# A gated cross-attention and mixture block on one core: attention's transposes moved up a step, the shared PSUM bank handed out in turn with a gap, and the mixture's transposes moved to other banks

## The chip, the core and the metric

The kernel runs on one NeuronCore of a Trainium2 chip. The metric is device time in microseconds (us) of one execution; the time before is 1071.58 us, the median of three runs (1070.88 to 1074.14). Five engines work side by side, each through its own list of instructions in a fixed order: TensorE (PE, matmul), VectorE (DVE), ScalarE (ACT), GpSimd (POOL) and SyncE (SP, which here issues nearly all DMAs). An instruction waits until what it reads is written and what it overwrites has been read; everything behind it in the same engine's list waits with it.

## What is computed

Eight sequences of 256 tokens with 512 features pass through two gated blocks in float32. The first is attention with 32 query heads, 8 key heads and a window of 64 tokens over two sources, the normed input and a context; one softmax runs over both. The second is a feed forward whose eight "basis" pieces are mixed per token with coefficients from a top-4 router, plus a shared part.

```python
x = x + tanh(g_xattn) * attention(layernorm(x), ctx)      # scores + alibi bias, masked to the window
xt = layernorm(x)
probs = softmax(xt @ w_router); topk_p, topk_idx = top_k(probs, 4)
basis = silu(xt @ w_gate) * (xt @ w_up)                   # 8 pieces of 256 columns
mixed = sum over experts and pieces of coeff * mix[topk_idx] * basis
out = mixed @ w_down + (silu(xt @ shared_w_gate) * (xt @ shared_w_up)) @ shared_w_down
x = x + tanh(g_ffn) * out
```

## The kernel before

One sequence is called b. Its work is four generators, and each `yield` hands back a cost. `project(b)` loads x and the context, norms x, transposes it in two halves (`tr_x`, L160), and makes keys (`pk`, L366), queries (`pq`, L385) and values (`pv`, L405). `attention(b)` has eight groups of scores; `score(i)` writes group i into four PSUM banks (`sc`, L444), one for each of four pairs of heads p. A group is worked off in two halves j; the running number of a half is u = 2i + j. `soften` (L457 on DVE, L466 on ACT) adds the bias, takes the maximum and exponentiates, once for each p. `divide` (a reciprocal L473 on DVE, four products L476 on POOL) normalises half u - 1, `turn` (L484 on DVE) transposes half u - 2 into `pt`, and `values` (L506) multiplies four turned halves with a block-diagonal copy of the values, `vbd`, into unused columns of score banks; `take` (L523, ACT) copies that out. `tail(b, t)` runs for each half t of the tokens: output projection `po` (L610), residual, norm, transposes `tr_f` (L160), router `pl` (L640), top-4 selection, `pst` (L672), `pc` (L680), which yields the mixing coefficients. `feed_forward(b)` does the eight pieces: plain products `gu` (L725) for b = 0, and for b > 0 seven half-size block products `m` (L788) in place of eight, from sums of weights kept in DRAM; then the shared part `ps` (L894), the transposes of the mixed result `pm` (L926) and the last product `pd` (L941).

The order of work is written by a small planner, not by the hardware: `start` gives a generator a time at which it begins (in units of one sequence) and a length; `run` always advances the one with the earliest time, and every instruction goes to its engine's list at that moment. In the steady state feed_forward(b), attention(b + 1), the tails of b + 1 and project(b + 2) are interleaved.

PSUM is shared out thus: four banks hold scores (`ps_sc`), three go round for the feed forward (`next_bank`), and one, `ps_one`, serves project (from b = 2 on), the tails and `pm` in turn. A generator that wants `ps_one` calls `hold` and yields until `held` is false. Since the bank is single, an instruction that writes the next tile into it waits for the one that reads the last tile out. For `tr_x` that reader is an ACT copy (L161), which stands in ACT's list among the exponentials of attention.

SP issues DMAs in list order: weight pieces `w` (L292), sixteen DMAs for `vbd` (L539) in each sequence, the output (L952).

Of the kernel before, what the change touches and what calls it, by code (L numbers as in the profile page):

```python
# [9 lines left out]
F32 = mybir.dt.float32  # L10
# [26 lines left out]
def gated_block(  # L37
# [43 lines left out]
        return ps_gu.tile([P, 2, T], F32, tag=f"gu{turns[0] % 3}", name=name)  # L81


    held = [False]

    def hold():
        while held[0]:
            yield 0.4
        held[0] = True


    loaded = {}
# [219 lines left out]

    AFTER, BEFORE = 1.8, 1.2
    projected = {}

    def project(b):
        def own():
            if b > 1:  # L320
                yield from hold()

        def bank(shape, name):
            if b > 1:
                return ps_one.tile(shape, F32, tag="one", name=name)

            flat = next_bank(name).rearrange("p a n -> p (a n)")
            if len(shape) == 2:
                return flat[:, : shape[1]]
            if len(shape) == 3:  # L330
                return flat.rearrange("p (a n) -> p a n", a=shape[1])
            return flat.rearrange("p (a b n) -> p a b n", a=shape[1], b=shape[2])

        def free():
            if b > 1:
                held[0] = False

        if b > 1:
            while b > 2 and b - 3 not in stored:
                yield 0.5  # L340
            loaded[b] = load(b), load_context(b)
            yield 16.0
        xt, ctT = loaded[b]
        if b == 0:
            xns = first_normed
        else:
            normed = norm(xt, range(NT), f"a{b}")
            yield 3.0
            xns = normed()
            yield 3.0  # L350
        xnT = two.tile([P, NC, T], F32, tag="xo", name=f"xnT_{b}")
        for t in range(NT):
            yield from own()
            evict = transposed(xnT, xns[t], t, f"x{b}", bank)
            yield AFTER
            evict()
            free()
            yield BEFORE


        kT = two.tile([P, 2, 2, T], F32, tag="kT", name=f"kT_{b}")
        yield from own()
        pk = bank([P, 2, T], f"pk_{b}")
        for s, (w_sb, src) in enumerate(((wsk_sb, ctT), (wk_sb, xnT))):
            for c in range(NC):
                nc.tensor.matmul(  # L366
                    pk[:, s, :], lhsT=w_sb[:, c, :], rhs=src[:, c, :],
                    start=(c == 0), stop=(c == NC - 1),
                )
            yield AFTER  # L370
        for par in range(2):
            for s in range(2):
                nc.scalar.activation(
                    kT[:, par, s, :], pk[:, s, :], AF.Copy, scale=kmask[:, par : par + 1],
                )
        free()
        yield BEFORE


        qT = two.tile([P, NB, G, Q], F32, tag="qT", name=f"qT_{b}")  # L380
        for g in range(G):
            yield from own()
            pq = bank([P, T], f"pq_{b}_{g}")
            for c in range(2 * NC):
                nc.tensor.matmul(  # L385
                    pq, lhsT=wq_sb[:, c, g * P : (g + 1) * P],
                    rhs=(ctT if c < NC else xnT)[:, c % NC, :],
                    start=(c == 0), stop=(c == 2 * NC - 1),
                )
                if c % NC == NC - 1:  # L390
                    yield AFTER
            nc.scalar.activation(
                qT[:, :, g, :], pq.rearrange("p (b q) -> p b q", q=Q), AF.Copy, scale=-0.25
            )
            free()
            yield BEFORE
        projected[b] = kT, qT


        yield from own()  # L400
        pv = bank([P, NT, 2, HK * D], f"pv_{b}")
        for t in range(NT):
            for s, (w_sb, src) in enumerate(((wsv_sb, ctT), (wv_sb, xnT))):
                for c in range(NC):
                    nc.tensor.matmul(  # L405
                        pv[:, t, s, :], lhsT=src[:, c, t * P : (t + 1) * P], rhs=w_sb[:, c, :],
                        start=(c == 0), stop=(c == NC - 1),
                    )
            yield AFTER
        nc.scalar.copy(  # L410
            vpad[:, :, D:].rearrange("p a (k r) -> p a k r", r=2 * D)[:, :, :, :D],
            pv.rearrange("p t s (k d) -> p (t s) k d", d=D),
        )
        free()
        yield BEFORE


    def attention(b):
# [112 lines left out]
        for u in range(2 * n + 4):  # L531
# [24 lines left out]
                nmax = small.tile([P, NPAIR], F32, tag="nmax", name=f"nm_{b}_{u}")  # L556
                dens[u] = small.tile([P, NPAIR], F32, tag="den", name=f"dn_{b}_{u}")
            yield 1.0
            for step, ps in enumerate(((0,), (1, 2), (3,))):
                for p in ps:  # L560
                    if i < n:
                        soften(i, j, p, scs, prs[u], nmax, dens[u])
                if step == 1 and j == 1 and m is not None:
                    take(m, scs)
                    if m == n // 4 - 1:
                        start(tail(b, 0, oT), 0.30, total=37.0)
                if step == 0 and 0 <= u - 1 < 2 * n:
                    divide((u - 1) // 2, (u - 1) % 2, prs[u - 1], dens.pop(u - 1))
                if step == 2 and 0 <= u - 2 < 2 * n:
                    k = (u - 2) // 4  # L570
                    if (u - 2) % 4 == 0:
                        pts[k] = two.tile(
                            [P, P // Q, NPAIR, COLS], F32, tag="pt", name=f"pt_{b}_{k}"
                        )
                    turn(u - 2, prs.pop(u - 2), pts[k])
                if u < 2 * n + 2:
                    yield 1.0 if i < n else 0.5
        start(tail(b, 1, oT), 0.31 if b > 0 else 0.26, total=37.0)
        yield 0.1


    hTs, coef = {}, {}

    sides = {}

# [14 lines left out]
    def tail(b, t, oT):  # L600
# [3 lines left out]
        n = f"{b}_{t}"  # L604
        xt, _ = loaded[b]
        yield 2.0
        yield from hold()
        po = bank([P, HID], f"po_{n}")
        for ch in range(4):
# [6 lines left out]
            out=xt[:, t, :], in0=po, scalar=tg[:, 0:1], in1=xt[:, t, :],  # L616
            op0=ALU.mult, op1=ALU.add,
        )
        held[0] = False
        normed = norm(xt, [t], f"f{b}")  # L620
        yield 2.5
        (xn,) = normed()
# [5 lines left out]
        evict = transposed(hT, xn, t, f"f{b}", bank)  # L628
        yield 2.5
        evict()  # L630
        held[0] = False
        yield 2.5
        if t == NT - 1 and b > 0:
            sides[b] = token_sums(b, hT)

# [13 lines left out]
        nc.gpsimd.memset(prob[:, E:], -1.0)  # L649
        den = small.tile([P, 1], F32, tag="rdn", name=f"rdn_{n}")  # L650
        nc.scalar.activation(prob[:, :E], pl, AF.Exp, bias=nmax, scale=1.0, accum_out=den)
        held[0] = False
        yield 2.5
        rden = small.tile([P, 1], F32, tag="rrd", name=f"rrd_{n}")
        nc.vector.reciprocal(rden, den)
# [17 lines left out]
        yield 2.5  # L673
        selT = one.tile([P, P], F32, tag="selT", name=f"selT_{n}")
        nc.scalar.copy(selT, pst)
        held[0] = False
        yield 1.5
        yield from hold()
        pc = bank([P, NK], f"pc_{n}")
# [1 line left out]
        yield 2.5  # L681
        cf = small.tile([P, NK], F32, tag="cf", name=f"cf_{n}")
        nc.vector.tensor_scalar(cf, pc, rts, None, op0=ALU.mult)
        held[0] = False
        coef[b, t] = cf
        yield 0.0

# [12 lines left out]
    def feed_forward(b):  # L700
        while b > 0 and b - 1 not in stored:
            yield 0.2
        hT = hTs[b]
        xt, _ = loaded.pop(b)
        mixed = [one.tile([P, I], F32, tag=f"mixed{t}", name=f"mixed_{b}_{t}") for t in range(NT)]
        ths, ups, todo = {}, {}, []

# [44 lines left out]
        if b == 0:  # L752

            order = [(0, 0), (1, 0), (0, 1), (1, 1)]
            order += [(k, t) for k in range(2, NK) for t in range(NT)]
            for k, t in order:
                plain(k, t)
                while len(todo) > 1:
                    todo.pop(0)()
# [21 lines left out]
            }  # L781
            weights_of = {1: (1, 0), 5: (1, 1), 2: (2, 0), 6: (2, 1), 7: (3, 0), 3: (4, 0), 4: (4, 1)}

        def product(k, m, dst, first=False):
            g, j = weights_of[m]
            w = wgu[b * PIECES + k, g]
            for c in range(NC // 2):
# [14 lines left out]

        def one_and_five(k):
            odd[k] = next_bank(f"m15_{b}_{k}")
            product(k, 1, odd[k][:, 0, :], first=True)
            product(k, 5, odd[k][:, 1, :])
            after(b * PIECES + k, 1)

        def keep_one_and_five(k):
# [2 lines left out]

        def seven_and_six(k):
            even[k] = next_bank(f"m76_{b}_{k}")
            product(k, 7, even[k][:, 0, :], first=True)
            product(k, 6, even[k][:, 1, :])
            after(b * PIECES + k, 3)

        def keep_seven(k):
# [4 lines left out]
            nc.gpsimd.tensor_add(m7, m7, tiles.pop(("m5", k)))  # L824

        def two_and_three(k):
            product(k, 2, odd[k][:, 0, :])
            product(k, 3, odd[k][:, 1, :])
            after(b * PIECES + k, 2)

        def first_tile(k):
# [2 lines left out]
            ths[k, 0] = silu2(bank[:, 0, :], f"th_{b}_0_{k}")  # L834

        def four(k):
            product(k, 4, even[k][:, 0, :])
            after(b * PIECES + k, 4)

        def second_gate(k):  # L840
# [48 lines left out]
        for ic in range(NSI):  # L889
# [29 lines left out]
            yield 3.46 if ic > 0 or b == 0 else 0.0  # L919
            if ic == 2:  # L920

                yield from hold()
                pm = ps_one.tile([P, NT, 2, P], F32, tag="one", name=f"pm_{b}")
                for t in range(NT):
                    for j in range(2):
                        nc.tensor.transpose(  # L926
# [1 line left out]
                        )  # L928
        mT = one.tile([P, NT, 2, P], F32, tag="mT", name=f"mT_{b}")
        nc.scalar.copy(mT, pm)  # L930
        held[0] = False
        act(*last)

        for t in range(NT):
# [19 lines left out]

    EARLY = -0.15
    active = []
    now = [0.0]

    def start(gen, length, at=None, total=8.0):

# [14 lines left out]
    with tc.manual_schedule():  # L977
# [3 lines left out]
        while 0 not in projected:  # L981
            next(chunks)
        coef_in = other_weights()
        now[0] = EARLY - 0.01
        for k, _ in enumerate(attention(0)):
            slot, at = divmod(k, 4)
            if at == 0 or (at == 2 and slot < 9):
                next(chunks, None)
# [3 lines left out]
                next(active[0][1], None)  # L992
        for _ in chunks:
            pass
        for b in range(B):
            if b + 1 < B:
                run(b + EARLY)
                start(attention(b + 1), 0.86, at=b + EARLY, total=71.0)
            run(float(b) if b > 0 else -0.1)
            start(feed_forward(b), b + 1.0 - now[0], total=73.2 if b > 0 else 80.6)  # L1000
            if b + 2 < B:
# [38 lines left out]
```

## Time and profile before

| | |
|---|---|
| median of the runs | 1071.58 us |
| the profiled execution | 1075.87 us, of which 1074.1 us are the profile's span |
| PE busy | 1017.0 us (95%) |
| DVE, ACT, POOL busy | 571.4, 413.6, 426.9 us |
| mean granted TensorE clock | 0.979 |
| instructions | 26137 |

A page of the profile gives busy time by engine, the span in 40 slices with the granted clock, the chain of work that ended last, and groups of instructions by line. Other views list who waited for whom, instructions in order of time, and busy time and clock in chosen stretches. A float32 matmul is two records in the trace, so counts there are twice those of the program. The busy time of PE holds matmuls that ran at half the clock, so it isn't a constant of the program.

### The profile page before, as it was taken

What the parts mean: (1) busy time and instruction counts of PE and PEld (TensorE: products, weight loads), DVE (VectorE), ACT (ScalarE), POOL (GpSimd) and SP (SyncE); (2) the same over time, 40 slices, a digit from 0 to 9 for tenths busy, and PEclk for the clock granted to TensorE, in tenths of its full rate; (3) what the DMA queues carried; (4) which work ended last, traced back from release to release, by engine and by line L of the source; (5) the groups of instructions that cost most, each with busy time, mean ns of one, the idle gap of its engine ahead of it and who ended that gap; (6) DMA issues with size and microseconds to landing.
All of it is one profiled execution on the core that took longest, in us unless ns stands there. A gap on an engine that the chain in (4) does not pass through costs nothing.

```text
span 1074.1 us, 26137 instructions
## 1 busy us (share of the span) xinstructions
PE 1017.0 (95%) x10032; PEld 802.1 (75%) x10032; DVE 571.4 (53%) x2164; ACT 413.6 (39%) x1578; POOL 426.9 (40%) x829
## 2 busy tenths in 40 slices
PE   6988889999999999999999999999999999999998
PEld 6766677866878678786878767886687867676885
DVE  1564565537655375554755357552665536673442
ACT  1553342315533255324544145431553325441220
POOL 3342665404534064432644136440454405550250
PEclk9898889999999999999999999999999999999999
DMA  9503864668643674447734296343854367552780
GB/s 289 153 2 78 307 207 154 220 187 246 187 138 110 159 265 142 132 129 197 256 118 139 87 255 210 119 138 112 262 185 133 117 151 232 177 184 84 261 287 21
DMA packets 97420, 183.37 MB, mean 171 GB/s; under 512 B 8720, under 2 KB 56336, under 8 KB 97296
## 3 DMA queue, kind: packets, MB, share of 16 engines
q1 hardware_dynamic: 95184, 179.87, 54.6%
q10 hardware_dynamic: 2112, 1.84, 0.5%
q8 instruction: 79, 1.29, 0.5%
q14 instruction: 45, 0.37, 0.1%
HBM read 146.02 MB, written 18.87 MB: 154 GB/s over the span
## 4 chain that ended last, share of the span: by engine, by line
PE 80%; DVE 8%; ACT 7%; issue 3%; POOL 1%; DMA 1%; SPq 0%; ACTq 0%; DVEq 0%; POOLq 0%
PE m L788 24%; PE pq L385 10%; PE ps L894 10%; PE pd L941 8%; PE sc L506 5%; PE sc L444 5%; PE po L610 5%; ACT pr L466 5%; PE gu L725 4%; PE pk L366 3%; PE pv L405 3%; DVE pr L457 2%; DVE pt L484 1%; PE pl L640 1%; DVE th L695 1%
## 5 line engine op out<-in xcount | busy, mean ns | idle before, releaser
L476 POOL TENSOR_SCALAR pr<-pr,rd 128x192 f32<-128x192 f32 (+2 forms) x512 | 207.3, 423 | 328.6 <-DVE rd L473 327.1
L466 ACT ACTIVATE pr<-pr,nm 128x192 f32<-128x192 f32 (+2 forms) x512 | 218.6, 428 | 296.0 <-DVE rd L473 164.1
L457 DVE CUSTOM_DVE_ANT_1 pr<-sc,nbias 128x192 f32<-128x192 f32 (+2 forms) x512 | 150.9, 324 | 165.3 <-PE sc L506 89.1
L788 PE MATMUL m<-w,sT 128*128 128x256 f32 x896 | 222.0, 380 | 0.0
L788 PEld LDWEIGHTS m<-w,sT 128*128 128x128 f32 x896 | 168.8, 190 | 23.5 <-issue 1.3
L788 PE MATMUL m<-w,hT 128*128 128x256 f32 x672 | 177.0, 386 | 0.0
L788 PEld LDWEIGHTS m<-w,hT 128*128 128x128 f32 x672 | 123.8, 191 | 20.6 <-issue 4.5
L894 PE MATMUL ps<-hT,w 128*128 128x256 f32 x512 | 121.0, 389 | 0.2 <-issue 0.2
L484 DVE STREAM_TRANSPOSE pt<-pr 128x768 f32<-128x768 f32 (+2 forms) x128 | 111.6, 872 | 1.8 <-POOL pr L476 1.8
L894 PEld LDWEIGHTS ps<-hT,w 128*128 128x128 f32 x512 | 97.8, 195 | 17.0 <-issue 3.9
L466 ACT ACTIVATION_READ_ACCUMULATOR pr<-pr,nm 128x1 f32 x512 | 96.3, 188 | 0.0
L823 POOL TENSOR_TENSOR m<-m,u 128x256 f32<-128x256 f32 x56 | 47.0, 839 | 111.1 <-DVE u L822 111.1
L853 POOL TENSOR_TENSOR mixed<-mixed,th 128x256 f32<-128x256 f32 x98 | 71.0, 725 | 50.1 <-DVE th L848 35.4
L506 PEld LDWEIGHTS sc<-pt,vbd 64*32 64x32 f32 x5120 | 61.2, 108 | 24.7 <-issue 15.7
L506 PE MATMUL sc<-pt,vbd 64*32 64x96 f32 (+2 forms) x5120 | 69.6, 232 | 7.6 <-issue 3.6
L444 PE MATMUL sc<-kT,qT 32*128 32x192 f32 (+2 forms) x1024 | 69.0, 346 | 6.9 <-DVE nm L457 6.7
L444 PEld LDWEIGHTS sc<-kT,qT 32*128 32x128 f32 x1024 | 47.5, 190 | 33.9 <-issue 20.1
L725 PE MATMUL gu<-w,hT 128*128 128x256 f32 x256 | 62.3, 400 | 2.9 <-DMA w<-in_L_ffn_w_gate 2.9
L385 PE MATMUL pq<-ctT,wq 128*128 128x256 f32 x256 | 62.2, 386 | 0.0
L385 PE MATMUL pq<-xnT,wq 128*128 128x256 f32 x256 | 60.7, 380 | 0.0
L941 PE MATMUL pd<-sd,shT 128*128 128x512 f32 x128 | 60.0, 592 | 0.0
L610 PE MATMUL po<-wo,oT 128*128 128x512 f32 x128 | 59.2, 605 | 0.5 <-ACT oT L523 0.5
(121 smaller groups left out, 1189.4 us busy)
## 6 DMA issues: line engine op xcount, KB each, us to landing
w<-s SPq DMA_DIRECT2D x168, 512.0 KB, 3.7
vbd<-vpad SPq DMA_DIRECT2D x128, 128.0 KB, 4.4
w<-s SPq DMA_DIRECT2D x56, 256.0 KB, 3.9
s<-w SPq DMA_DIRECT2D x24, 512.0 KB, 5.8
w<-in_L_ffn_shared_w_gate SPq DMA_DIRECT2D x16, 512.0 KB, 3.8
w<-in_L_ffn_shared_w_up SPq DMA_DIRECT2D x16, 512.0 KB, 3.7
x<-in_x SPq DMA_DIRECT2D x8, 512.0 KB, 5.2
ctT<-in_ctx SPq DMA_DIRECT2D x8, 512.0 KB, 6.3
```

Source lines behind the costliest of these rows:

```text
L385: nc.tensor.matmul(pq, lhsT=wq_sb[:, c, g * P : (g + 1) * P], rhs=(ctT if c < NC else xnT)[:, c % NC, :], start=(c == 0), stop=(c == 2 * N ...
L444: nc.tensor.matmul(seen(scs[p][:, j * COLS : (j + 1) * COLS], qb), lhsT=qT[rows, qb].rearrange("p g q -> p (g q)"), rhs=kT[rows, par, :, f ...
L457: nc.vector.tensor_tensor_reduce(out=part, in0=seen(scs[p][:, j * COLS : (j + 1) * COLS], qb0 + j), in1=bass.AP(tensor=bias.tensor, offset ...
L466: nc.scalar.activation(part, part, AF.Exp, bias=nmax[:, p : p + 1], scale=-1.0, accum_out=den[:, p : p + 1],)
L476: nc.gpsimd.tensor_scalar(part, part, rden[:, p : p + 1], 1.0, op0=ALU.mult, op1=ALU.mult)
L484: nc.vector.transpose(pt[:, u % 4].rearrange("p c (s k) -> p (c s) k", s=2)[:, :, lo:], pr.rearrange("p c (s k) -> p (c s) k", s=2)[:, :, ...
L506: nc.tensor.matmul(scs[gp][32 * c : 32 * (c + 1), 2 * COLS + lo * Q : 2 * COLS + hi * Q], lhsT=vbd[rows, kb % (P // Q), kb // (P // Q) * 2 ...
L610: nc.tensor.matmul(po, lhsT=oT[:, ch // 2, ch % 2, t * P : (t + 1) * P], rhs=wo_sb[:, ch % 2, ch // 2, :], start=(ch == 0), stop=(ch == 3),)
L725: nc.tensor.matmul(pg[:, j, :], lhsT=hT[:, c, t * P : (t + 1) * P], rhs=(lower if c < NC // 2 else upper)[:, 0, c % (NC // 2), :], start=( ...
L788: nc.tensor.matmul(dst, lhsT=sides_of[m][c], rhs=w[:, j, c, :], start=(first and c == 0), stop=(c == NC // 2 - 1), skip_group_check=True,)
L894: nc.tensor.matmul(pg[:, j, :], lhsT=w[:, c, ic % 2 * P : (ic % 2 + 1) * P], rhs=hT[:, c, :], start=(c == 0), stop=(c == NC - 1),)
L941: nc.tensor.matmul(po, lhsT=lhsT, rhs=rhs, start=(j == 0), stop=(j == len(inner) - 1))
```

## The change

The same instructions are issued, only in another order, and `pm` writes to another bank. In each half of attention the four softens stood as (0), (1, 2), (3) in three steps, with `take` in the second and `turn` in the third; they now stand as (0), (1), (2, 3), and `turn` and then `take` are in the second step. The last steps of attention, which have no softens, yield 0.8 in place of 0.5. `hold` is a queue, first come first served, and the bank is given on only when 0.007 of a sequence has passed on the planner's clock since it was given back; project yields 0.8 in place of 1.2 after giving back. `pm` takes a bank of the feed forward's three. Attention starts at -0.2 of a sequence in place of -0.15 (still -0.15 for the first) and its units are counted as 74.1 in place of 71. A tail's second half waits for the first half's transposes, and the feed forward for the transposes and token sums that it reads.

```diff
-    held = [False]
+    queue = []
+    given = [-1.0]
+    now = [0.0]
+    GAP = 0.007
     def hold():
-        while held[0]:
+        me = object()
+        queue.append(me)
+        while queue[0] is not me or now[0] < given[0] + GAP:
             yield 0.4
-        held[0] = True
+    def give():
+        queue.pop(0)
+        given[0] = now[0]
...
-    AFTER, BEFORE = 1.8, 1.2
+    AFTER, BEFORE = 1.8, 0.8
...
-            for step, ps in enumerate(((0,), (1, 2), (3,))):
+            for step, ps in enumerate(((0,), (1,), (2, 3))):
                 for p in ps:
                     if i < n:
                         soften(i, j, p, scs, prs[u], nmax, dens[u])
-                if step == 1 and j == 1 and m is not None:
-                    take(m, scs)
-                    if m == n // 4 - 1:
-                        start(tail(b, 0, oT), 0.30, total=37.0)
                 if step == 0 and 0 <= u - 1 < 2 * n:
                     divide((u - 1) // 2, (u - 1) % 2, prs[u - 1], dens.pop(u - 1))
-                if step == 2 and 0 <= u - 2 < 2 * n:
+                if step == 1 and 0 <= u - 2 < 2 * n:
...
                     turn(u - 2, prs.pop(u - 2), pts[k])
+                if step == 1 and j == 1 and m is not None:
+                    take(m, scs)
+                    if m == n // 4 - 1:
+                        start(tail(b, 0, oT), 0.30, total=37.0)
                 if u < 2 * n + 2:
-                    yield 1.0 if i < n else 0.5
+                    yield 1.0 if i < n else 0.8
...
+        while t > 0 and (b, t - 1) not in turned:
+            yield 0.4
         yield from hold()
         po = bank([P, HID], f"po_{n}")
...
+        turned.add((b, t))
...
+        while (b, 0) not in turned or b > 0 and b not in sides:
+            yield 0.2
...
-                yield from hold()
-                pm = ps_one.tile([P, NT, 2, P], F32, tag="one", name=f"pm_{b}")
+                pm = next_bank(f"pm_{b}").rearrange("p t (j n) -> p t j n", j=2)
...
-    EARLY = -0.15
+    EARLY, FIRST = -0.2, -0.15
...
-                run(b + EARLY)
-                start(attention(b + 1), 0.86, at=b + EARLY, total=71.0)
+                at = b + (EARLY if b > 0 else FIRST)
+                run(at)
+                start(attention(b + 1), 0.86, at=at, total=74.1)
```

All places that set `held[0] = False` call `give()` instead; the one after `pm` is gone. `product` is renamed `block`, and the clock in the loop over the first attention is counted upwards.

More of the change, by code (lines that the diff above doesn't have):

```diff
@@ L335, in free @@
             if b > 1:
-                held[0] = False
+                give()
         if b > 1:
@@ L575, in attention @@
                     turn(u - 2, prs.pop(u - 2), pts[k])
+                if step == 1 and j == 1 and m is not None:
+                    take(m, scs)
+                    if m == n // 4 - 1:
+                        start(tail(b, 0, oT), 0.30, total=37.0)
                 if u < 2 * n + 2:
-                    yield 1.0 if i < n else 0.5
+                    yield 1.0 if i < n else 0.8
         start(tail(b, 1, oT), 0.31 if b > 0 else 0.26, total=37.0)
         yield 0.1
-    hTs, coef = {}, {}
+    hTs, coef, turned = {}, {}, set()
     sides = {}
@@ L618, in tail @@
         )
-        held[0] = False
+        give()
         normed = norm(xt, [t], f"f{b}")
@@ L630, in tail @@
         evict()
-        held[0] = False
+        give()
         yield 2.5
+        turned.add((b, t))
         if t == NT - 1 and b > 0:
@@ L651, in tail @@
         nc.scalar.activation(prob[:, :E], pl, AF.Exp, bias=nmax, scale=1.0, accum_out=den)
-        held[0] = False
+        give()
         yield 2.5
@@ L675, in tail @@
         nc.scalar.copy(selT, pst)
-        held[0] = False
+        give()
         yield 1.5
@@ L683, in tail @@
         nc.vector.tensor_scalar(cf, pc, rts, None, op0=ALU.mult)
-        held[0] = False
+        give()
         coef[b, t] = cf
@@ L702, in feed_forward @@
             yield 0.2
+        while (b, 0) not in turned or b > 0 and b not in sides:
+            yield 0.2
         hT = hTs[b]
-        xt, _ = loaded.pop(b)
+        xt, _ = loaded[b]
         mixed = [one.tile([P, I], F32, tag=f"mixed{t}", name=f"mixed_{b}_{t}") for t in range(NT)]
@@ L756, in feed_forward @@
             for k, t in order:
+                while (b, t) not in turned:
+                    yield 0.2
                 plain(k, t)
@@ L782, in feed_forward, with block @@
             weights_of = {1: (1, 0), 5: (1, 1), 2: (2, 0), 6: (2, 1), 7: (3, 0), 3: (4, 0), 4: (4, 1)}
-        def product(k, m, dst, first=False):
+        def block(k, m, dst, first=False):
             g, j = weights_of[m]
@@ L804, in one_and_five @@
             odd[k] = next_bank(f"m15_{b}_{k}")
-            product(k, 1, odd[k][:, 0, :], first=True)
-            product(k, 5, odd[k][:, 1, :])
+            block(k, 1, odd[k][:, 0, :], first=True)
+            block(k, 5, odd[k][:, 1, :])
             after(b * PIECES + k, 1)
@@ L814, in seven_and_six @@
             even[k] = next_bank(f"m76_{b}_{k}")
-            product(k, 7, even[k][:, 0, :], first=True)
-            product(k, 6, even[k][:, 1, :])
+            block(k, 7, even[k][:, 0, :], first=True)
+            block(k, 6, even[k][:, 1, :])
             after(b * PIECES + k, 3)
@@ L826, in two_and_three @@
         def two_and_three(k):
-            product(k, 2, odd[k][:, 0, :])
-            product(k, 3, odd[k][:, 1, :])
+            block(k, 2, odd[k][:, 0, :])
+            block(k, 3, odd[k][:, 1, :])
             after(b * PIECES + k, 2)
@@ L836, in four @@
         def four(k):
-            product(k, 4, even[k][:, 0, :])
+            block(k, 4, even[k][:, 0, :])
             after(b * PIECES + k, 4)
@@ L930, in feed_forward @@
         nc.scalar.copy(mT, pm)
-        held[0] = False
         act(*last)
@@ L953, in feed_forward @@
         stored.add(b)
-    EARLY = -0.15
+    EARLY, FIRST = -0.2, -0.15
     active = []
-    now = [0.0]
     def start(gen, length, at=None, total=8.0):
@@ L983, in gated_block @@
         coef_in = other_weights()
-        now[0] = EARLY - 0.01
         for k, _ in enumerate(attention(0)):
+            now[0] = FIRST - 0.01 * (72 - k)
             slot, at = divmod(k, 4)
@@ L994, in gated_block @@
             pass
+        now[0] = FIRST
         for b in range(B):
             if b + 1 < B:
-                run(b + EARLY)
-                start(attention(b + 1), 0.86, at=b + EARLY, total=71.0)
+                at = b + (EARLY if b > 0 else FIRST)
+                run(at)
+                start(attention(b + 1), 0.86, at=at, total=74.1)
             run(float(b) if b > 0 else -0.1)
```

## The prediction

> **What bounds the kernel now.** First the page's busy times and its chain: PE is busy for 95% of the span and holds 80% of the chain that ended last. So only two things can move the time by much: how long PE stands still, and at what clock it runs.
>
> ```profile
> PE 1017.0 (95%) x10032; PEld 802.1 (75%) x10032; DVE 571.4 (53%) x2164; ACT 413.6 (39%) x1578; POOL 426.9 (40%) x829
> PE 80%; DVE 8%; ACT 7%; issue 3%; POOL 1%; DMA 1%; SPq 0%; ACTq 0%; DVEq 0%; POOLq 0%
> ```
>
> Next the waits of PE over the whole span (total, times, longest):
>
> ```profile
> PE tr_x L160 <- DVE xn_a L146: 8.1, 1, 8.1
> PE sc L444 <- DVE nm L457: 6.7, 11, 1.3
> PE tr_f L160 <- DVE xn_f L146: 5.7, 3, 3.6
> PE pl L640 <- ACT hT L161: 5.6, 7, 1.3
> PE pc L680 <- ACT selT L675: 5.5, 8, 1.4
> PE pv L405 <- ACT prob L651: 4.1, 5, 1.7
> PE tr_x L160 <- ACT xnT L161: 4.0, 5, 2.1
> PE sc L506 <- issue: 3.6, 2, 1.8
> ```
>
> Some 53 us in all, 8 of them the first load. Asked for one steady sequence (379 to 505 us), the same view has 1.1 (pc, two boundaries), 0.7 (pl), 0.6 (pv), 0.5 (tr_x), 0.3 (sc): under 3 us in 126. Last, stretches with the granted clock, which follow the start and end (PE busy is the second figure, PEclk the third from the end):
>
> ```profile
> 598.00:601.40 3.40, 1.55 (x97) 1.30 (x94) 0.46 (x2) 0.17 (x2) 0.72 (x1) 1.00 0.03 7
> 601.40:604.80 3.40, 3.40 (x9) 2.73 (x9) 0.00 (x0) 0.27 (x2) 0.00 (x0) 0.51 0.02 5
> 123.60:130.40 6.80, 5.83 (x14) 4.66 (x15) 3.08 (x13) 1.65 (x8) 5.02 (x5) 0.50 0.86 270
> 147.50:154.30 6.80, 4.75 (x22) 3.71 (x15) 5.44 (x20) 3.39 (x13) 4.58 (x7) 0.50 0.74 285
> ```
>
> A wait of 1.85 us in a stretch was followed by 3.4 us at half clock, which costs 1.7 us more.
>
> **The change, part by part.** The lists of the two built programs hold the same instructions on every engine, so nothing is added or removed; I set the orders side by side and price each place where a producer and its consumer come closer or part. Durations: a 128x256 matmul takes 0.4325 us (eight records in 1.73 us in the chain), a 128x512 one 0.86, a group of scores 0.86, four transposes 0.53.
>
> *Sequence boundary, b = 1 to 5.* Now: po_1, ps_1, pc_0, ps_2, tr_f_1, scores 0, pm, ps_3, pl_1, pd_0, scores 1, pst_1, pd_1, pc_1, scores 2. pl_1 is 4 us behind tr_f_1, which ends its 0.72 us wait; pc_1 has all of pd_1 (5.2 us) before it, which ends 0.56. tr_f_1 has 7 us after po_1, and the chain po, residual, norm, POOL power, xn took 3.3 us (480.24 to 483.54), so it is covered. pm's own bank costs nothing: ps_3 now needs ps_1's bank, read out during ps_2 and scores 0. But SP limits this place:
>
> ```profile
> 488.19 11.61 SPq L539 DMA_DIRECT2D vbd<-vpad  x16
> 499.90 0.54 SPq L952 DMA_DIRECT2D out<-x  x1
> 500.54 1.22 SPq L292 DMA_DIRECT2D w<-s  x2
> ```
>
> SP's order is unchanged: after ps_3 (ends 487.58) come sixteen vbd DMAs, the output, then the third weight piece, which lands about 3.5 us after its issue, at ps_3 + 16.4. Before, PE first needed it at 504.97, ps_3 + 17.4. Now scores 0, tr_f_1 and pm lie ahead of ps_3 and two waits are gone: pl 0.9, pd_0 5.15, scores 1 0.86, pst 0.2, pd_1 5.15, pc 0.3, scores 2 0.7, four matmuls 1.73 make ps_3 + 15.0. So 1.5 us of new wait (1.0 to 1.9), inside which scores 2 waits too (its last two banks are freed by softens that stand behind cf_1 on DVE, after pc_1). Net of 0.72 + 0.56 + 0.33: 0.1 us gained each, 0.5 in all.
>
> *tr_x, b = 1 to 5: the place that decides.* Before, the order is tr_x_0, scores 4, two matmuls, tr_x_1; ACT's copy of tr_x_0 stands right behind the first exponential of scores 4. tr_x_1 can't write the bank before that copy:
>
> ```profile
> 401.23 0.60 PE L160 MATMUL tr_x<-ident,xn_a 128*128 128x128 f32 x4
> 401.76 0.93 PE L444 MATMUL sc<-kT,qT 32*128 32x192 f32 x16
> 402.62 1.13 PE L788 MATMUL m<-w,hT 128*128 128x256 f32 x4
> 404.24 0.66 PE L160 MATMUL tr_x<-ident,xn_a 128*128 128x128 f32 x4 [0.49 <-ACT xnT L161]
> ```
>
> Attention now runs earlier: scores 4, fourteen matmuls, tr_x_0, two matmuls, tr_x_1, scores 5. On ACT the copy stands behind all eight exponentials of scores 4. PE reaches tr_x_1 at 0.86 + 14 x 0.4325 + 0.53 + 0.87 = 8.3 us after scores 4 begins. DVE's list from the last soften of group 3 to the last of group 4 has eight softens, two turns, two reciprocals, two norm statistics, two xn and seven feed-forward operations: the same as before between groups 2 and 3, which took from 390.22 to 400.44:
>
> ```profile
> 390.22 0.29 DVE L457 CUSTOM_DVE_ANT_1 pr<-sc,nbias 128x128 f32<-128x128 f32 x1
> ...
> 400.44 0.35 DVE L457 CUSTOM_DVE_ANT_1 pr<-sc,nbias 128x192 f32<-128x192 f32 x1
> ```
>
> That is 10.2 us, plus 0.5 because both turns are now full size (0.97, one was 0.44): 10.7. Group 3's last soften ends some 0.4 us before scores 4 begins (8 us of DVE work against 8.5 us of PE), so group 4's last one begins at 10.3 and ends at 10.6. Its exponential comes second of two (1.0 with the reads of the sums), the copy takes 0.56, hand-over 0.1: 12.2. So tr_x_1 waits 3.9 us (3.0 to 4.6) where it waited 0.49: 5 x 3.4 = 17 us lost. Queued behind it on PE are scores 5, the values and the rest of the feed forward; nothing covers them.
>
> *The clock after it.* The row above says that 1.85 us of standing still cost 3.4 us at half speed. [...] I take the window for all five tr_x, 5 x 1.7 = 8.5 us (0 to 17, for none or two windows each), and none for the boundary (up to 5 x 1.7).
>
> *Smaller places, b = 1 to 5.* pv now follows pst with values and four matmuls between, and its 0.62 us goes: 3.1 gained. pq_2 comes 2.9 us after tr_f_0, whose copy stands behind four exponentials: about 0.4 each, 2 lost.
>
> *Values 3.* Its two halves were split only by pc, and PE stood still inside for 1.85 and 1.72 us at 598.7 and 728.6 ("issue": the profile shows no releaser), each with a half-clock window: 3.6 + 3.4 = 7.0. Now four matmuls (1.73 us) lie between. No row says what such a stop depends on; bounds are 0 and 7.0 gained, and I take 7, for it came only in the dense double run.
>
> *First sequence (100 to 252 us).* POOL's weight sums of piece 0 now stand ahead of tail 1's norm in its list, where POOL idled 12 us; scores 1 comes 5 us earlier. So the last sum follows gu_1_0 directly (115.6, not 119.2), and the weights that PE awaited for 2.85 us land 3.5 us sooner. With this wait, the 3.1 us that the clock took at 123.6, 1.3 of tr_x_1's 2.05 (its copy stands behind two exponentials that are long done), half of the clock loss at 147.5 (1.7), and 0.8 at the end: 10.4. Against it pl_1 and pc_1 have no cover (0.7 and 0.6). Net 9 gained (4 to 13).
>
> *Last sequence (890 to 1074).* Between scores 6 and 7 PE has 7.4 us, DVE 11: 3.6 lost plus a clock window 1.7; gone are 1.31 with its window (1.7) at 920 us and 1.47 of tr_f_0, and 0.3 more comes to pc_1. Net 1 lost.
>
> *The first attention* keeps PE's order to 95 us; the turn ahead of two softens moves each by under 1 us either way: 0.
>
> Sum: 17 + 8.5 + 2 + 1 - 0.5 - 3.1 - 7 - 9 = **+8.9 us**, so 1075.87 + 8.9 = 1084.8 for a profiled execution. That one stood 4.3 us above the median of the runs, so I say **1080.5 us**.
>
> **Rivals.** (1) *Faster.* All gains without tr_x come to 16.6 us, so the change pays if tr_x_1's wait stays under 0.49 + 16.6/5 - 1.7 = 2.1 us. For it: DVE idled over 1 us in the 10.2 us that I copied. Against it: the wait on PE would have to be nearly halved. With 1.3 us and no clock window: 5 x 0.8 - 16.6 = -12.6, 1059 us. (2) *Two clock windows* after each tr_x, and stops inside values elsewhere: +8.5 + 7, 1096 us. For it: two windows followed the waits at 121 and 148 us. (3) *SP becomes the bound*: if vbd's DMAs are late, as they were at 492 (1.4 us between two issues), each boundary loses 1.5 more with a clock window: +16, 1096 us. (4) *The orders matter nothing*, since PE is busy anyway: 1071.6. Against it: the waits above change place by place.
>
> **Chances.** Likeliest case 0.60 (own range 1070 to 1091), rival 1 0.19, rivals 2 and 3 together 0.16, rival 4 0.05. A measurement tells about 0.3%, 3.2 us, from no change. Faster 0.20, same 0.06, slower 0.74. The range 1060 to 1100 leaves out a tenth at each end.
>
> **What would show it.** Right: PE's wait for ACT's xnT grows from 4.0 us to about 20, half-clock stretches follow each, waits of pl and pv nearly vanish, a wait of m for the weights w appears at the boundaries, no stop inside values 3, no wait of gu for DMA. Wrong: if xnT waits stay under 10 us, or if stops inside values stay.

## The result, and the profile after

The changed kernel takes 1108.28 us (median of four runs, 1106.84 to 1111.03), the kernel before on the same chip 1071.63 us: a ratio of 1.0349, 95% interval 1.0317 to 1.0381. It is slower, as forecast, but by 36.7 us and not 9, and outside the range of 1060 to 1100. The profiled execution took 1109.11 us, 33.2 us more than that of before, which stood 4.3 us above its median; that of the changed kernel stands 0.8 above. What is read from the two traces below is a part of the 33.2 us.

The page of the changed kernel, busy times and chain (its lines from `project` on stand nine to sixteen lines lower than before: `tr_x` is L169, scores L453, ACT's copies of the transposes L170):

```profile
PE 1035.4 (94%) x10032; PEld 817.1 (74%) x10032; DVE 573.0 (52%) x2164; ACT 415.8 (38%) x1578; POOL 425.5 (38%) x829
PE 72%; DVE 11%; ACT 8%; DMA 4%; issue 2%; SPq 2%; POOL 0%; ACTq 0%; DVEq 0%; POOLq 0%
```

PE does the same instructions and is busy for 18.4 us more. The trace of the changed kernel has 74.6 us at half clock, of which PE is busy for 63.8; that of before has 48.0 and 40.4. Work done at half clock took twice as long (before, 32 records of `gu` took 10.04 us with 5.8 us of half clock in them, where two groups of 16 at full clock make 7.1), so half of the difference, 11.7 us, is the clock's; the other 6.7 us are not placed. The remaining 15 us are standing still. Its waits (total, times, longest):

```profile
PE tr_x L169 <- ACT xnT L170: 19.5, 6, 3.8
PE sc L453 <- DVE nm L466: 9.9, 21, 1.8
...
PE pc L692 <- ACT selT L687: 5.4, 5, 2.5
PE m L804 <- DMA w<-s: 5.2, 5, 1.9
PE pq L394 <- ACT kT L382: 3.5, 5, 0.9
...
PE sc L515 <- issue: 1.3, 1, 1.3
```

`tr_x`'s wait for the copy was 4.0 us and is 19.5. The waits of `pv` are gone and those of `pl` are down from 5.6 to 2.5 us; these gains are small beside it. The place itself, one sequence, all engines in order of time (start, duration, instruction):

```profile
401.43 0.59 PE L453 MATMUL sc<-kT,qT 32*128 32x192 f32 x4
...
409.47 0.60 PE L169 MATMUL tr_x<-ident,xn_a 128*128 128x128 f32 x4
...
413.07 0.35 DVE L466 CUSTOM_DVE_ANT_1 pr<-sc,nbias 128x192 f32<-128x192 f32 x1
...
414.08 0.56 ACT L170 COPY xnT<-tr_x 128x512 f32<-128x512 f32 x1
...
414.69 1.11 PE L169 MATMUL tr_x<-ident,xn_a 128*128 128x128 f32 x4 [3.76 <-ACT xnT L170]
```

The last soften of scores 4 begins 11.64 us after the scores; two exponentials later the copy runs, and the second half of `tr_x` begins at 414.69. And the clock around another of these waits (stretches of 3.41 us; PE busy is the second figure, the granted clock the third from the end):

```profile
806.01:809.43 3.42, 3.42 (x19) 2.98 (x17) 3.30 (x12) 1.79 (x7) 0.94 (x2) 1.00 0.91 329
809.43:812.84 3.41, 1.25 (x8) 0.79 (x6) 2.84 (x12) 1.36 (x5) 3.27 (x6) 1.00 0.60 183
812.84:816.25 3.41, 1.82 (x12) 1.49 (x16) 1.66 (x7) 2.31 (x8) 1.36 (x3) 0.50 0.37 137
816.25:819.67 3.42, 3.42 (x79) 2.72 (x76) 1.26 (x6) 0.80 (x3) 0.64 (x2) 0.50 0.02 5
```

One wait of 3.76 us is spread over two stretches (2.16 and 1.59 us idle). The clock is halved in the second of them already, and in the one after it. So it was in four of the five sequences; the fifth had one such stretch.

### The profile page after: what moved, and what is told of

Read it like the earlier page. It is cut to its first block, busy times and chain, and to the rows that moved or that the text cites. A ratio compares the mean times of both kernels' runs of the same rounds, so it can differ in the third digit from the quotient of the medians.

```text
span 1107.3 us, 26165 instructions
## 1 busy us (share of the span) xinstructions
PE 1035.4 (94%) x10032; PEld 817.1 (74%) x10032; DVE 573.0 (52%) x2164; ACT 415.8 (38%) x1578; POOL 425.5 (38%) x829
## 3 DMA queue, kind: packets, MB, share of 16 engines
q10 hardware_dynamic: 2112, 1.84, 0.5%
q8 instruction: 79, 1.29, 0.5%
## 4 chain that ended last, share of the span: by engine, by line
PE 72%; DVE 11%; ACT 8%; DMA 4%; issue 2%; SPq 2%; POOL 0%; ACTq 0%; DVEq 0%; POOLq 0%
PE m L804 21%; PE ps L910 10%; PE pq L394 9%; PE sc L515 5%; PE po L621 5%; PE sc L453 5%; PE pd L955 5%; ACT pr L475 4%; PE gu L739 4%; DMA w<-s 3%; PE pk L375 3%; DVE pr L466 3%; PE pv L414 3%; DVE pt L493 2%; DVE th L707 2%
## 5 line engine op out<-in xcount | busy, mean ns | idle before, releaser
L485 POOL TENSOR_SCALAR pr<-pr,rd 128x192 f32<-128x192 f32 (+2 forms) x512 | 202.3, 414 | 303.2 <-DVE rd L482 231.3
L804 PE MATMUL m<-w,sT 128*128 128x256 f32 x896 | 228.8, 390 | 5.2 <-DMA w<-s 5.2
L804 PEld LDWEIGHTS m<-w,sT 128*128 128x128 f32 x896 | 174.4, 196 | 32.4 <-DMA w<-s 7.2
L910 PE MATMUL ps<-hT,w 128*128 128x256 f32 x512 | 117.5, 381 | 0.0
L910 PEld LDWEIGHTS ps<-hT,w 128*128 128x128 f32 x512 | 95.2, 190 | 14.7 <-issue 2.9
L453 PE MATMUL sc<-kT,qT 32*128 32x192 f32 (+2 forms) x1024 | 80.0, 364 | 10.4 <-DVE nm L466 9.9
L453 PEld LDWEIGHTS sc<-kT,qT 32*128 32x128 f32 x1024 | 56.4, 201 | 35.8 <-DVE nm L466 16.7
L838 DVE TENSOR_TENSOR u<-u,m 128x256 f32<-128x256 f32 x56 | 23.6, 421 | 70.2 <-ACT m L837 69.6
```

What stands on the lines that cost most here:

```text
L453: nc.tensor.matmul(seen(scs[p][:, j * COLS : (j + 1) * COLS], qb), lhsT=qT[rows, qb].rearrange("p g q -> p (g q)"), rhs=kT[rows, par, :, f ...
L485: nc.gpsimd.tensor_scalar(part, part, rden[:, p : p + 1], 1.0, op0=ALU.mult, op1=ALU.mult)
L804: nc.tensor.matmul(dst, lhsT=sides_of[m][c], rhs=w[:, j, c, :], start=(first and c == 0), stop=(c == NC // 2 - 1), skip_group_check=True,)
L910: nc.tensor.matmul(pg[:, j, :], lhsT=w[:, c, ic % 2 * P : (ic % 2 + 1) * P], rhs=hT[:, c, :], start=(c == 0), stop=(c == NC - 1),)
```

## Experiments

All ratios are against the kernel before, run beside it on the same chip. Line numbers in the fences are those of each kernel.

### Which part of the change

Attention's time, set back in the changed kernel:

```diff
-    EARLY, FIRST = -0.2, -0.15
+    EARLY, FIRST = -0.15, -0.15
...
-                start(attention(b + 1), 0.86, at=at, total=74.1)
+                start(attention(b + 1), 0.86, at=at, total=71.0)
```

> The changed kernel with the start and the length of attention set back (-0.15 of a sequence and 71.0). The two halves of tr_x then stand behind values 1 again, with scores 4 between them, as in the kernel before. Theory A (the loss is tr_x_1's wait for ACT's copy and the half clock behind it, and the earlier attention is what puts it there): the five waits of 3.76 us fall to under 1 us and the half-clock stretches behind them vanish, 5 x (3.2 + 3.2) = 32 us; two waits of about 1 us per boundary may come back: 1077 to 1087 us. Theory B (the queue for the shared bank and its gap lose the time, wherever attention stands): above 1098 us.

Measured: 1090.62 us, ratio 1.0169 (1.0134 to 1.0204). `tr_x` waits 0.57 us in each of the five sequences and no half clock follows. But the time is 3.6 us above what theory A had. Two things in its trace bear on that: `pk` waits 1.20 us for the copy of the second half in five sequences (the order has only four matmuls between) and `pc` 1.16, as allowed for; and PE stopped three times for 2.98, 3.80 and 3.79 us with no releaser, each with a half-clock stretch or two.

The steps of a half, set back in the changed kernel:

```diff
-            for step, ps in enumerate(((0,), (1,), (2, 3))):
+            for step, ps in enumerate(((0,), (1, 2), (3,))):
...
-                if step == 1 and 0 <= u - 2 < 2 * n:
+                if step == 2 and 0 <= u - 2 < 2 * n:
...
                     turn(u - 2, prs.pop(u - 2), pts[k])
```

(and `take` before `divide` again).

> The changed kernel with the steps of a half of attention as before: (0), (1, 2), (3), take in the second, turn in the third. TensorE's order in the steady state is the same as in the changed kernel. Theory A: the last two softens of a half no longer stand behind a turn of 0.97 us, so the exponentials ahead of tr_x's copy end some 0.5 to 1 us sooner: tr_x_1 waits 2.8 to 3.3 us instead of 3.76, and the first attention gets back 1 to 3 us: 1100 to 1106 us. Theory C (the turn in the middle is what makes tr_x wait): the waits fall under 1 us and the time under 1090 us. Rival: no change, 1107 to 1109.

Measured: 1089.58 us, ratio 1.0165 (1.0122 to 1.0209), with TensorE's order in the steady state untouched. The time falls just inside theory C's range, but not for theory C's reason: the five waits of `tr_x` are 3.13 us, as theory A says, and not under 1 us. What theory A did not say is what 0.63 us less does to the clock: 13.6 us of half clock behind the five waits, where the changed kernel had 30.7. (The profiled execution is the fastest of the four, 1084.65 us at a granted clock of 0.980; the others had 0.973 to 0.978, so more half clock.) Two of the five were followed by none:

```profile
661.66:665.07 3.41, 1.69 (x9) 1.00 (x7) 2.84 (x15) 1.31 (x6) 2.70 (x5) 1.00 0.68 196
665.07:668.49 3.42, 1.97 (x66) 1.58 (x69) 2.24 (x6) 2.27 (x9) 1.94 (x5) 1.00 0.47 152
668.49:671.90 3.41, 3.41 (x52) 3.02 (x41) 1.34 (x9) 2.16 (x8) 1.63 (x4) 1.00 0.28 65
```

The rest lies ahead of the steady state. When the project of the third sequence begins its keys (156.3 us before), this kernel is 6.9 us ahead of the kernel before; the changed kernel is 1.4 us behind it.

Both set back in the changed kernel (what is left is the queue, its gap, project's shorter wait, the 0.8 in attention's last steps, `pm`'s bank and the guards):

> The changed kernel with both undone: attention's start and length, and the steps of a half. What is left of the change is the queue with its gap, the shorter wait of project, pm's own bank and the guards. Theory A (two causes that add: the earlier attention costs tr_x's wait and clock in the steady state, the turn costs the first attention and part of tr_x's wait): against the run with the steps alone undone the five tr_x waits of 3.13 us and their half clock go (some 20 us), waits of pk (1.2) and pc (1.2) come in five or six sequences (12 us), and the dense double values may bring their stops back (5 to 15 us): 1075 to 1092 us. Theory B (the rest of the change is what is good, and it beats the kernel before): below 1068 us.

Measured: 1079.69 us, ratio 1.0086 (1.0053 to 1.0119): theory A. Theory B falls: what is left of the change is no gain by itself, with 13.5 us of waits of `pc`, 5.6 of `pk`, and three stops of 1.5 to 3.4 us. So the four kernels make a table (medians in us; the kernel before had 1070.7 to 1072.6 beside them):

| | steps as before | steps as changed |
|---|---|---|
| attention's time as before | 1079.7 | 1090.6 |
| attention's time as changed | 1089.6 | 1108.3 |

Each costs about 10 us alone and both 28.6: 7.8 us more than their sum. Taken from the ratios it is 10.8 us, and the intervals of the four ratios together leave it between about 3 and 19 us. The half clock that the longer wait adds, (30.7 - 13.6) / 2 = 8.5 us at most, is of that size; that it is the whole excess is not shown.

The steps alone, in the kernel before (the same edit the other way):

> The kernel before with one part alone: the steps (0), (1), (2, 3), turn and then take in the second. TensorE's order in the steady state is that of the kernel before. Theory A (turn ahead of the last two softens holds up PE where DVE has no slack, so in the first attention, the first sequence and the last): 5 to 12 us slower, 1077 to 1085 us, with scores waiting for softens up to 150 us and the steady sequences within 0.5 us each. Rival (turn earlier is harmless by itself, and costs only in the queue's order): 1070 to 1074 us.

Measured: 1080.58 us, ratio 1.0089 (1.0062 to 1.0115): theory A, and the place that theory A named. Its profiled execution is 5.3 us behind when the second `po` runs (97.3 us before) and still 4.6 us behind at 591 us; the steady sequences gain or lose under 0.5 us each, up to where stops differ. (The profiled executions end 4.8 us apart, the medians 9.9: that of before lies 4.3 us above its median.)

Attention's time alone, in the kernel before:

> The kernel before with one part of the change alone: attention starts at -0.2 and is counted as 74.1. tr_x_0 then stands ten matmuls behind scores 4, and tr_x_1 behind scores 5 and values. Theory A: tr_x_1 or the scores ahead of it wait 3 us or more in five sequences, with half clock behind: 1090 to 1108 us. Theory B: under 1080 us, since without queue and gap nothing is lost.

Measured: 1118.63 us, ratio 1.0444 (1.0397 to 1.0491), slower than the whole change. Theory B is wrong, and theory A is wrong about the place: `tr_x` waits 1.55 us, for DVE's norm, and the loss is spread over many waits, for weights, for DVE's norm and for the readers of the one shared bank:

```profile
PE tr_x L160 <- DVE xn_a L146: 15.8, 6, 8.1
PE m L788 <- DMA w<-s: 12.8, 6, 3.1
PE pq L385 <- ACT hT L161: 10.3, 6, 2.5
...
PE pq L385 <- ACT kT L373: 6.4, 5, 1.3
PE pm L926 <- ACT prob L651: 6.1, 5, 1.2
```

8.1 of the first line is the first load, as always. The granted clock was 0.983, above the 0.979 of before: this loss is standing still, of which there are 37 us more than before. `pm` waiting for `prob` and `pq` for `hT` are instructions that take `ps_one` right behind another owner. In the changed kernel those of `pm` are absent and those of `pq` are 0.3 to 0.4 us. With the earlier attention, then, the rest of the change is a gain: 1118.6 us here, 1089.6 with queue, gap and `pm`'s bank added and the steps left alone. Without it, it is a loss of 9. Queue, gap and bank were not tried apart.

### What the wait costs, and why

Work put into the wait: eight matmuls on zeros between the halves, in the five sequences (`between` is set when the first half is issued and cleared with the second; `zeros` is a tile of zeros, so the products add zero to `four`'s sum).

```diff
+            if between[0]:
+                for _ in range(8):
+                    nc.tensor.matmul(
+                        even[k][:, 0, :], lhsT=sides_of[4][0], rhs=zeros,
+                        start=False, stop=True, skip_group_check=True,
+                    )
```

> The changed kernel with eight matmuls more between tr_x_0 and tr_x_1 in the five sequences where tr_x_1 waits: they add a product with zeros to a bank that is being summed, 8 x 0.4325 = 3.5 us of work that fits in the wait of 3.76 us. Nothing is left out. If the half clock behind the wait comes from TensorE standing still, the four stretches of 6.8 us and the one of 3.4 us behind these waits vanish and the time falls by about 15 us, to 1091 to 1096 us, though more work is done. If it comes from something else (from the work that follows, or from the load of the chip), the time stays at 1107 to 1111 us.

Measured: 1092.35 us, ratio 1.0211 (1.0167 to 1.0254): 16 us less than the changed kernel in the medians, 15 by the ratios, with 17.3 us more work.

```profile
535.27 1.03 PE L808 MATMUL m<-w,hT 128*128 128x256 f32 x4
536.13 3.62 PE L860 MATMUL m<-zeros,hT 128*128 128x256 f32 x16
540.06 0.65 PE L169 MATMUL tr_x<-ident,xn_a 128*128 128x128 f32 x4 [0.31 <-ACT xnT L170]
```

`tr_x_1` begins when it would have begun anyway, and between 107 and 950 us this trace (the fastest of the four executions, 1088.43 us) has no half clock at all. The half clock behind the wait comes from standing still.

Half of it filled (`range(4)`):

> As the run with the filled wait, with four matmuls on zeros in place of eight: 1.73 us of the 3.76 are filled, a wait of 2.0 us stays. The traces so far show half clock on a fixed grid of 3.413 us, after a grid window in which TensorE stood still for more than about 1.9 us. Theory G (the grid window decides): a wait of 2.0 us falls into one window or is split between two, so one to three of the five waits are followed by half clock, by one window each: 2 to 5 us above the filled run, 1094 to 1098 us. Theory R (each wait over 1.85 us is followed by a window): five windows, 8.5 us, 1100 to 1103 us. Theory S (only gaps over about 3 us): none, 1091 to 1093 us.

Measured: 1099.71 us, ratio 1.0269 (1.0235 to 1.0304). The five waits are 2.03 us each, and none is followed by half clock in the profiled execution. Theory R falls. Theory G gave one to three; by its own rule none was due, since each wait was split and no window held more than 1.80 us of idle (here 0.88 and 1.15):

```profile
540.51:543.93 3.42, 2.54 (x12) 1.90 (x10) 2.85 (x13) 1.73 (x6) 3.34 (x7) 1.00 0.78 267
543.93:547.34 3.41, 2.27 (x84) 1.84 (x84) 1.22 (x3) 1.95 (x8) 0.92 (x2) 1.00 0.15 56
```

By this trace alone theory S holds as well; it falls by waits of 1.85 and 1.72 us that were followed by half clock (the kernel before, so that theory G's 1.9 us was set too high) and by the 3.13 us above that were not. The time agrees less well: it is 7.4 us above the filled run (6.2 by the ratios), where theory G says 2 to 5. In the profiled executions the difference is 9.4 us, and it lies elsewhere: this one has 6.8 us of half clock at 124 us and 13.6 after 930, where the filled run has none and 3.4, which makes (20.4 - 3.4) / 2 = 8.5 us. Why those two places fell otherwise was not tried.

One value back, so that scores 5 and values stand between the halves of `tr_x`:

```diff
-    AFTER, BEFORE = 1.8, 0.8
+    AFTER, BEFORE = 1.8, 1.2
```

> The changed kernel with one value back: project yields 1.2 instead of 0.8 after it gives the bank back. Scores 5 and values then stand between tr_x_0 and tr_x_1. Theory A (what is late is DVE, with the softens of scores 4; the copy on ACT only waits for them): the wait does not go, it moves to scores 5, which need the banks that these softens read: scores wait 2 to 2.7 us there in pieces, tr_x_1 under 0.6 us, pq's wait of 0.65 for kT goes, and half clock follows in fewer of the five places: 1085 to 1097 us. Theory D (only the place of the copy in ACT's list is at fault): with 1.7 us more work ahead of tr_x_1 the waits nearly vanish, and the time is under 1082 us.

Measured: 1090.09 us, ratio 1.0184 (1.0169 to 1.0200), inside theory A's range. The wait moved on to the scores, which need the banks that the late softens read:

```profile
412.43 0.59 PE L453 MATMUL sc<-kT,qT 32*128 32x192 f32 x2 [0.60 <-DVE nm L466]
413.57 1.19 PE L453 MATMUL sc<-kT,qT 32*128 32x192 f32 x12 [0.56 <-DVE nm L466]
...
415.52 0.66 PE L169 MATMUL tr_x<-ident,xn_a 128*128 128x128 f32 x4
```

So the softens of scores 4 are what is late; ACT's copy only stands behind them. Cut into pieces, the wait is smaller (1.2 us in waits over 0.5, where 2 to 2.7 was expected) and half clock follows it in three of five places, one stretch each, after only 0.77 to 1.16 us idle in the window before. One more point missed: `pq`'s wait for `kT` did not go, it is 0.8 us.

### A version that beats both

From the run with both set back, the order was opened where it still waited:

```diff
-    GAP = 0.007
+    GAP = 0.010
...
         nc.scalar.copy(selT, pst)
         give()
-        yield 1.5
+        yield 3.5
```

> The same as the run with both undone, but with the gap at 0.010 of a sequence in place of 0.007 and 3.5 in place of 1.5 yielded between pst and pc. The order then has six matmuls and scores 4 between the halves of tr_x, scores 1 between tr_f_1 and pl_1, eight matmuls or more between pst_1 and pc_1, pk behind four matmuls, and work between the two dense halves of values 3. Theory A: none of the waits that these places had remains above 0.6 us, no stops inside values 3, and the first sequence keeps the 7 to 9 us that it gains where turn is back: 1055 to 1066 us, faster than the kernel before. Rival (PE's waits only move on to the next wait for DVE, since a sequence has too little slack): 1068 to 1080 us.

Measured: 1067.37 us, ratio 0.9963 (0.9943 to 0.9983): 0.4% faster than before, with an interval that leaves out 1, and 1.4 us above what theory A had. The places opened wait at most 0.8 us in the steady state. The stops were not gone: 0.57, 1.56 and 1.60 us in values 3 or just behind, with half clock after two of them.

The same, with attention's last steps yielding 0.5 (half of `pv` now stands between the dense halves of values 3), and with 1.4 (`ps_2` does):

> As the run with the wider gap, with 0.5 yielded again in attention's last steps. The two dense halves of values 3 then have half of pv (eight 128x128 matmuls, about 1 us) between them instead of pst, and ps_1 and ps_2 lie behind them. Stops inside values 3 have come with a transfer of 16 KB of instructions in flight after a dense run of small matmuls. Theory F (the stops depend on how many small matmuls stand close together): with this little between them two or three stops of 1.5 to 3 us remain, and the time is that of the wider gap within 3 us, 1064 to 1071 us. Rival (any order with other work between is enough): no stop over 0.5 us and two or three half-clock windows less, 1056 to 1062 us.

> As the run with the wider gap, with 1.4 yielded in attention's last steps in place of 0.8. The two dense halves of values 3 then have ps_2 (3.5 us of sixteen-record matmul groups) between them; pst_1 comes only scores and four matmuls behind pl_1. Theory F: no stop over 0.6 us inside values 3. pst_1 has 2.6 us of work ahead of it where its chain on DVE needs about 5, so it waits 2 to 3 us in each of six boundaries, sometimes with half clock behind it: 1070 to 1084 us. Rival (stops come whatever lies between): stops of 1.5 us or more remain in two or three sequences.

Measured: 1062.50 us, ratio 0.9936 (0.9917 to 0.9954), and 1066.00 us, ratio 0.9960 (0.9948 to 0.9973). In its profiled execution, the fastest of six (1060.24 us, clock 0.989; the slowest had 0.982), the first has no stop above 0.3 us and no half clock between 149 us and the last microsecond: the rival's case, though its median is half a microsecond above the rival's range. The second has no stop at values 3 in the steady state (one of 1.64 us at 221 us, in the first sequence); its `pst` waits at most 1.0 us where 2 to 3 were expected, so it lands below the range. Theory F asked for too much: eight matmuls of `pv` were enough here, as the sixteen-record groups of `ps_2` were; with a single `pst` or `pc` between there were stops. Each of these is one profiled execution, and the runs with the filled wait and with project's wait back had no stop over 0.5 us either, so part of the difference may be chance.

## Why the prediction was wrong

By its own terms, from the two profiled executions (b = 1 to 5 where nothing else is said):

| step of the prediction | predicted | measured |
|---|---|---|
| `tr_x_1`'s wait | +17 | +16.8: five of 3.76 us, four of 0.49 gone |
| the clock after it | +8.5 | +13.2: 30.7 us at half clock, less 4.3 us idle in them, by 2 |
| boundary | -0.5 | -1.2 |
| `pv` | -3.1 | -4.1 |
| `pq_2` | +2 | +1.6 |
| `pq_0` behind `pk` | not seen | +3.5: four waits of 0.65 us, one of 0.93 |
| values 3 | -7 | -5.7: a stop of 1.32 us came elsewhere |
| first attention | 0 | +6.5 at the second `po` |
| first sequence after it | -9 | -4.7 |
| last sequence | +1 | about +4, three of them clock |
| sum | +8.9 | +30; 3 of the 33.2 us are not placed |

The 21 us between the two sums lie in five rows: the first attention (6.5), the clock (4.7), the first sequence (4.3), `pq_0` (3.5) and the last sequence (3); the other rows nearly cancel.

**The wait was right**, place, releaser and size. The size was luck in part: the copied distance of 10.3 us between the scores and the last soften was 11.6, and PE's way to `tr_x_1` was 9.5 us and not 8.3, since scores 4 wait for their own banks and take 1.9 us and not 0.86. The two errors cancel (12.2 - 8.3 forecast, 13.2 - 9.5 found).

**The clock term was mis-sized.** "I take the window for all five tr_x, 5 x 1.7 = 8.5 us" counted one window of half clock for each wait, from a row with a wait of 1.85 us. Four of five had two. What failed is that the loss was taken per wait, not by how the wait falls into the windows (below). For the boundary it took none, a choice that no run had tested: the trace before has waits of 1.31, 1.66 and 1.73 us (at 241, 333 and 967 us) with no half clock behind them, and one of 1.31 us (at 920) with it. It held: none of `m`'s five waits in the changed kernel, 0.51 to 1.87 us, was followed by half clock.

**"The turn ahead of two softens moves each by under 1 us either way: 0" failed.** It priced one soften and not their sum, nor the clock. Up to the second `po` (97 us before) the changed kernel has 2 us more waits of PE (scores 0.63 and 0.39, 0.56 for `take`'s copy, `pst` and `pc` 0.9 together), 6.8 us more of half clock (3.4 us), and a first group of `pk` that took 1.2 us longer. The last is no effect of the change: in the other eleven traces it took between 2.59 and 3.62 us, and 2.40 before. The run with the steps alone, 5.3 us behind at the same place, shows the cause. In the changed kernel:

```profile
40.98 0.68 PE L453 MATMUL sc<-kT,qT 32*128 32x64 f32 x2 [0.63 <-DVE nm L466]
65.05 1.19 PE L453 MATMUL sc<-kT,qT 32*128 32x192 f32 x12 [0.39 <-DVE nm L466]
71.22 1.61 PE L453 MATMUL sc<-kT,qT 32*128 32x192 f32 x16 [0.56 <-ACT oT L532]
```

**The first sequence's -9 was right for the change without its steps**: from the second `po` to the third sequence's keys, the run with the steps set back gains 8.5 us (from 1.6 behind to 6.9 ahead). With the steps as changed, the wait for weights vanished as said and `tr_x_1`'s fell to 0.68, but scores then waited for softens at 123 and 144 us (1.62 and 1.84 us, against 1.18 before). Part of the gain was given back to DVE. Two sums of the prediction are also off, without weight: its terms for this sequence add to 9.75 as listed and not 10.4, and the waits listed for one steady sequence to 3.2 us and not under 3.

**`pq_0` was missed** because project's 0.8 in place of 1.2 was read only as a distance between the halves of `tr_x`, not between `pk`, its copies and `pq_0`.

The prediction's rival 2 named the two windows, at 1096 us; without the first attention's loss and the smaller misses it also falls short. Rival 1's break-even of 2.1 us was never near, and rival 3's late DMAs did not come: `m` waited 0.5 to 1.9 us, as the boundary's sum had it.

## What to carry to other kernels

On a PE that is busy for 95%, price a new wait twice: its length, and the half clock behind it (here 16.8 and 13.2 us for five waits of 3.76 us). Before anything else shorten it until no window of 3.41 us holds 0.6 us of it (of some 3450 windows below that none was followed by half clock, of 284 with 0.6 to 1.7 us 27 were), or fill it with matmuls (eight in each of the five took 15 to 16 us off the time). When two edits lengthen the same wait, their costs need not add (here about 10 us each and 28.6 together): test them as a two by two table. An edit on an engine off the chain (here a transpose put two softens earlier on DVE, 0.9% slower by itself and 5.3 us behind at the second `po`) is to be priced at the places with the least slack, start and end, not in the steady state.

## What the runs showed of the hardware

**Half clock came in windows of a fixed grid.** In each of the thirteen traces all half-clock stretches begin on multiples of 3.413 us from one origin. In the changed kernel's they begin at 38.02, 82.39, 96.04, 147.24, 283.78, 413.48, 546.60, 679.72 and 812.84 us and at four later places; the eight given behind the first lie 13, 17, 32, 72, 110, 149, 188 and 227 times 3.4133 us from it. The origin differs from execution to execution: counted from the start of the span it lies at 0.47 us there and at 0.70 in the trace before. PE's idle time in each grid window at full clock, after 30 us, counted in the clock and matmul records of the traces:

| idle in the window | all thirteen: windows, followed by half clock | before and changed alone |
|---|---|---|
| under 0.6 us | some 3450, 0 | 526, 0 |
| 0.6 to 1.7 us | 284, 27 | 41, 5 |
| 1.7 to 2.0 us | 31, 20 | 8, 6 |
| over 2.0 us | 52, 52 | 9, 9 |

After 200 us, a window already at half clock was followed by another wherever it held 0.37 us idle or more (7 of 7; in the two traces 4 of 4), and never with less than 0.2 (0 of 44; 0 of 11): so 3.76 us got two. This explains each case here: 1.85 us inside one window was followed by half clock, 2.03 us split into 0.88 and 1.15 was not, 3.13 us was or wasn't, as it fell, and 3.76 us can't be split so that both parts stay below 1.8. In the run with project's wait back 0.77 to 1.16 us were enough three times; those windows held scores, matmuls on 32 rows. The same holds over all thirteen traces: with 0.6 to 1.7 us idle, half clock followed 25 of the 109 windows with at least six records of scores, and 2 of the 175 others (5 of 17 and 0 of 24 in the two traces). That matmuls on 32 rows count for less is a guess that fits; no run tested it.

**PE stopped in runs of small matmuls, close to transfers on the instruction queue.** Over the thirteen traces there are 19 stops of over 0.5 us that the profile calls "issue", 16 in the values and three at the `po` right behind them; the longest took 3.80 us (attention's time set back). Before each, 155 to 221 matmul records ran in 10 us, and a transfer of 16 KB on the instruction queue ended 0.9 to 1.6 us before PE went on. For the stops of 1.85 and 1.72 us in the trace before it was 199 and 220 records, and 1.29 and 1.53 us; for the one of 1.32 us in the changed kernel's, 172 records and 1.45 us. The two together are not enough: each trace has 79 such transfers, and some 300 of those without a stop of over 0.5 us came in runs as dense (20 of 77 in the trace before). That the transfer is the cause is argued from this coincidence and from the stops' absence where larger matmuls stood between the dense halves; it wasn't tested by itself, and what sets the 19 apart from the rest is open.
